# Counting SyncE's row fetches on one semaphore per batch, and giving SyncE 16 batches to fetch in place of 12

## The chip, the cores and the metric

The kernel runs on one core of a Trainium2 chip. A core has a matrix engine (TensorE, PE in the profile; its weight loads are PEld), a vector engine (VectorE, DVE), an activation engine (ScalarE, ACT), GpSimd (POOL) and SyncE (SP), which computes nothing and issues transfers. Each engine works through a list of instructions in the order in which they were written, and engines wait for one another through semaphores. ScalarE, SyncE and GpSimd can issue DMA transfers; the transfers of all three run on the core's 16 DMA engines. The metric is the device time of one execution in microseconds (us); lower is better.

## The reference

A layer of a graph network: 12,500 nodes with 160 features each, 400,000 edges, sorted by destination. The part that matters here is the gather of a mapped node row for each edge, the product with weights that each edge computes for itself, and the sum by destination.

```python
h = jnp.maximum(_layernorm(x, axis=-1), 0.0)
y0 = x0 @ W_l1_0 * a * inv0                       # y: one row of 160 floats per node
y1 = jnp.einsum('nuc,uv->nvc', x1, W_l1_1) * a[:, :, None] * inv1
w = silu(edge_length_embedded @ fc_W1 / 4) @ fc_W2 / 8    # weights of each edge
ys0 = y0[edge_src]                                # the gather
ys1 = y1[edge_src]
mid_a = w_a * ys0 * e0
mid_b = (w_b * ys0)[:, :, None] * e1[:, None, :]
...
z0 = jnp.zeros((n, MID)).at[edge_dst].add(mid0) * inv_nb
out = x + concat(C_S * s0 + C_X * (z0 @ W_l2_0) * a / sqrt(MID), ...)   # s0: the node's own path
```

## The kernel before, in words

A first stage maps all nodes and writes the rows to `y_d` in HBM. Then the main loop goes over the edges in 782 batches (`NB`) of 4 tiles (`GT`) of 128 edges, so a batch needs 512 rows of `y_d`, 640 bytes each. The loop takes almost all of the time. For each batch PE computes the edges' weights (L689), DVE builds the selection of destinations (L704, L706) and the products of weights and rows (L573, L577), and PE sums the products by destination (L720).

The order of every engine's instructions is the order in which the program text issues them (`manual_schedule`); nothing is moved afterwards. So a batch's steps stand on each engine in the order of the loop body, and an engine that waits holds up all that stands behind it.

The rows of a batch come in one of four ways:

- GpSimd fetches them with four indirect gathers, one for each tile (L615), into a ring of 6 buffers (`yg`). This is the way of most batches.
- 18 batches (`XB`), one in every 43 (`PER`), get raw features early and are mapped again on PE (`x_center`, `x_turn`, `x_map`), in the 18 slots of the buffer `xr`. A slot is free for other use once its x batch is done.
- SyncE fetches all 512 rows of a batch one by one: each row is one small DMA from `y_d` into the slot (`row_fetch_by_sp`, L638), whose address SyncE reads from SBUF into registers, 32 at a time (`row_places`, L626, one TENSOR_LOAD). The table `jobs` says which batches. A job starts in batch `s`, spreads its 16 chunks of 32 rows over the next `RB` = 58 batches, and its rows are used 7 batches after that; the next job starts `RB` after the one before. 12 jobs.
- ScalarE does the same in units of 8 rows, one unit at the end of a batch's steps (`row_fetch_by_act`); its jobs stand `AB` = 66 apart. 10 jobs.

SyncE also issues the loads of edge features `xe` (L407, two every 8 batches), of edge attributes and indices `raw`, `src_q`, `dst_q` (L415 to L419) and one store `drel_d` (L433) every 24 batches, and of the nodes' own features `xs` for the nodes' own path (L766, three in every 43 batches). These stand in the same list as the row fetches. DVE reads `xs` at L773 (`skip_center`), five batches behind the load's place in the program at the closest.

Semaphores: the framework counts a DMA of SyncE or ScalarE in one of eight *lanes* (DMAHW0 to DMAHW7), taken in turn; a DMA waits until the one before it in its lane has landed. ScalarE's rows are excepted already: they count on a semaphore of their own for each batch (`came`, `no_tile_sem_insts`, `add_to_no_dep_group`), and DVE waits for that semaphore's full count (`all_rows`) ahead of the batch's first product. SyncE's rows use the lanes.

Of the kernel before, what the change touches and what calls it, by code (L numbers as in the profile page):

```python
# [12 lines left out]
U8 = mybir.dt.uint8  # L13
# [9 lines left out]
D = M0 + 3 * M1  # L23
# [20 lines left out]
LATE = 8  # L44
XB = 18
SK = 9
RB = 58
RS = 30
AB = 66
AS = 102  # L50
RN = 32
AN = 16
RU = 8
# [7 lines left out]
def kernel(  # L61
# [19 lines left out]
    nc = tc.nc  # L81
# [10 lines left out]
    for q, w in enumerate(wts_of):  # L92
        gstart.append(len(glist))
        n = min(BLK, T - q * BLK)
# [9 lines left out]
    y_b = y_d.rearrange("n c -> (n c)").bitcast(U8)  # L104
# [51 lines left out]
    NX = P * GT // RN  # L156
    jobs = [(s, RB, True) for s in range(RS, NB - 1 - RB - 7, RB)]
    jobs += [(s, AB, False) for s in range(AS, NB - 1 - AB - 7, AB)]
    jobs = [(s, s + m + 7, m, by_sp) for s, m, by_sp in sorted(jobs)]
# [420 lines left out]
    with (  # L580
# [10 lines left out]
        hids, rows, wts, sels, z_ps, zT, o_sb, prs, sums_ps, summed = ({} for _ in range(10))  # L591
        xss, hss, sTs, sps, ohs, ohTs, vals, xTs = ({} for _ in range(8))
        halves, came, places_of = {}, {}, {}
# [30 lines left out]
        def row_places(j, n, m, engine):  # L624
            q, o = divmod(n, P // RP * GT)
            _, places = nc.values_load_multi_w_load_instructions(  # L626
                ri[RP * j + q:RP * j + q + 1, o:o + m], engines=[engine], min_val=0, max_val=(N - 1) * D * 4,
                skip_runtime_bounds_check_because="places of nodes, as the indices of the other fetches")
            return places

        def row_fetch(j, n, eng, places):
            b = jobs[j][1]
            if n == 0:
                rows[b] = xr[:, slot_of[j], :, :]
            fetches = []
            for m, v in enumerate(places):
                e, k = divmod(n + m, GT)
                fetches.append(eng.dma_start(rows[b].bitcast(U8)[e:e + 1, k, :], y_b[ds(v, D * 4)].unsqueeze(0)))  # L638
            return fetches

        def row_fetch_by_sp(j, n):
            row_fetch(j, RN * n, nc.sync, row_places(j, RN * n, RN, mybir.EngineType.SP))

        def row_fetch_by_act(j, n):
            o = RU * n % AN
            if n == 0:
                came[jobs[j][1]] = tc.alloc_semaphore(f"rows_{j}"), f"rows_{j}"
            sem, group = came[jobs[j][1]]
            for fetch in row_fetch(j, RU * n, nc.scalar, places_of[j][o:o + RU]):
                fetch.then_inc(sem, 16)  # L650
                tc.no_tile_sem_insts.add(fetch.ins.name)
                tc.add_to_no_dep_group(group, fetch.ins)

        def act_places(j, n):
            if RU * n % AN == 0:
                places_of[j] = row_places(j, RU * n, AN, mybir.EngineType.Activation)

        def all_rows(b):
            if b in came:
                sem, group = came[b]  # L660
                tc.declare_fence(nc.vector.wait_ge(sem, 16 * P * GT).ins, group=group)
# [289 lines left out]
        for b in range(NB):  # L951
            g = group_of[b]
            k = b - first_of[g]
# [9 lines left out]
            u, v = divmod(b, PER)  # L963
# [3 lines left out]
            if units and units[0][0] <= b:  # L967
                act_places(*units[0][1:])
# [27 lines left out]
            if units and units[0][0] <= b:  # L996
                row_fetch_by_act(*units.pop(0)[1:])
# [12 lines left out]
    with (  # L1010
# [4 lines left out]
        n = nc.values_load(far_i[0:1, 0:1], min_val=0, max_val=1)  # L1015
        with tc.For_i(0, n, 1) as _:
# [77 lines left out]
            with tc.For_i(0, NT, 1) as i:  # L1094
# [4 lines left out]
                for c in range(3):  # L1099
                    o = 256 + 64 * c  # L1100
# [62 lines left out]
```

## Time and profile before

| | |
|---|---|
| median of 3 runs | 4903.42 us |
| lowest, highest | 4900.01, 4938.69 us |
| the profiled execution | 4914.76 us |
| its span in the profile | 4912.9 us |
| busy: PE, DVE, POOL, ACT | 3930.2, 2747.3, 2878.2, 609.6 us |
| rows fetched by SyncE, by ScalarE | 6144, 5120 |
| gathers by GpSimd (L615) | 2965 |

The profile names work by engine and by line of the kernel before. A row of the view of waits gives who waited for whom, the total in us, how often, and the longest. A row of the timeline gives the start in us, the length in us, the engine (SPq and ACTq are the parts of SyncE and ScalarE that issue transfers), the line, the operation and how many instructions of it were merged.

### The profile page before, as it was taken

The numbers are of one execution on the slowest core, as the hardware profiler recorded it, in microseconds if no ns is written. First come the engines' busy times: TensorE is split into PE (matmuls) and PEld (weight loads), VectorE is DVE, ScalarE is ACT, GpSimd is POOL, SyncE is SP. The second block draws the span as 40 slices with busy tenths as digits, with TensorE's granted clock in tenths as the row PEclk, the third lists the DMA queues.
The fourth block names the chain that finished last, engine by engine and source line by source line (L and its number), as shares of the span: only waits on it lengthen the run. The fifth ranks groups of instructions, "written<-read, shape, count | busy, mean of one in ns | idle before, by whom it ended". The sixth has DMA issues, their size and how long they took to land. (4 is left out here: it accounts for less than half of the span.)

```text
span 4912.9 us, 76368 instructions
## 1 busy us (share of the span) xinstructions
PE 3930.2 (80%) x17274; PEld 2517.5 (51%) x17274; DVE 2747.3 (56%) x6901; ACT 609.6 (12%) x1863; POOL 2878.2 (59%) x3045
## 2 busy tenths in 40 slices
PE   7778887767778686887777787888887888888888
PEld 7444544444445454554454555555554555555555
DVE  5455555544555454555455565566565666666666
ACT  5011011101101010111011111111111111111110
POOL 6666665646656565555556556566556555565654
PEclk8889898878989898988899898899898888999889
DMA  7222222222222222222222222222222222222223
GB/s 194 67 69 64 70 66 64 60 55 65 65 57 65 58 66 59 64 61 61 56 64 65 63 57 66 61 67 64 64 60 64 61 65 61 65 63 62 65 61 109
DMA packets 272510, 330.52 MB, mean 67 GB/s; under 512 B 84288, under 2 KB 223456, under 8 KB 272048
## 3 DMA queue, kind: packets, MB, share of 16 engines
q0 software_dynamic: 145776, 248.99, 20.5%
q1 hardware_dynamic: 115408, 73.03, 5.3%
q10 hardware_dynamic: 10864, 3.57, 0.4%
q8 instruction: 140, 2.29, 0.2%
q14 instruction: 322, 2.64, 0.2%
HBM read 307.72 MB, written 17.61 MB: 66 GB/s over the span
## 5 line engine op out<-in xcount | busy, mean ns | idle before, releaser
L615 POOL DMA_INDIRECT yg<-y_d,src_q x2965 | 2808.5, 947 | 1962.4 <-issue 702.5
L720 PE MATMUL pz<-pr,sel 128*128 128x320 f32 x6250 | 2122.9, 486 | 51.4 <-issue 23.2
L720 PEld LDWEIGHTS pz<-pr,sel 128*128 128x128 f32 x6250 | 1244.4, 210 | 726.2 <-issue 384.3
L689 PE MATMUL pw<-w,hT 64*128 64x192 f32 x6250 | 825.4, 387 | 331.4 <-DVE pr L577 168.3
L689 PEld LDWEIGHTS pw<-w,hT 64*128 64x128 f32 x6250 | 567.4, 210 | 632.0 <-issue 512.1
L726 DVE STREAM_TRANSPOSE za<-pz 128x160 f32<-128x160 f32 x598 | 206.2, 345 | 1050.5 <-PE pz L720 443.5
L577 DVE TENSOR_TENSOR pr<-pw,yg 128x384 f32<-128x384 f32 x1484 | 749.4, 546 | 0.0
L706 DVE TENSOR_TENSOR sel<-own,pw 128x512 f32<-128x512 f32 x782 | 536.8, 686 | 28.3 <-DVE own L704 1.4
L573 DVE TENSOR_TENSOR pr<-pw,yg 128x512 f32<-128x512 f32 x742 | 506.2, 682 | 9.3 <-DMA yg<-y_d,src_q 9.3
L704 DVE TENSOR_TENSOR own<-iota,pw 128x128 f32<-128x128 f32 x782 | 204.8, 262 | 511.2 <-issue 265.3
L668 PE MATMUL px<-xe,w 32*128 32x512 f32 x782 | 442.1, 648 | 40.5 <-issue 15.9
L568 ACT ACTIVATE pw<-ev 128x20 f32<-128x20 f32 x782 | 149.2, 191 | 2472.6 <-DMA xr<-y_d 526.1
L673 ACT ACTIVATE hT<-px 128x512 f32<-128x512 f32 x391 | 233.2, 597 | 972.4 <-remote 220.5
L733 PEld LDWEIGHTS px<-wo,za 128*128 128x128 f32 x1500 | 227.4, 203 | 153.2 <-issue 77.6
L733 PE MATMUL px<-wo,za 128*128 128x160 f32 x1500 | 261.5, 325 | 53.0 <-issue 11.9
L668 PEld LDWEIGHTS px<-xe,w 32*128 32x128 f32 x782 | 115.6, 185 | 220.0 <-issue 180.4
L745 PE MATMUL px<-os,place 128*128 128x160 f32 x600 | 127.7, 340 | 116.6 <-ACT os L735 94.6
L727 DVE STREAM_TRANSPOSE za<-pz 32x160 f32<-32x160 f32 x598 | 202.0, 338 | 21.6 <-DVE za L726 1.2
L780 PE MATMUL px<-ident,sh 128*128 128x128 f32 x98 | 31.7, 341 | 219.7 <-DVE sh L773 180.3
L745 PEld LDWEIGHTS px<-os,place 128*128 128x128 f32 x600 | 100.0, 209 | 163.2 <-ACT os L735 114.5
L773 DVE TENSOR_SCALAR sh<-xs,mv 128x160 f32<-128x160 f32 x98 | 26.5, 309 | 251.9 <-DMA xs<-in_x 251.9
L780 PEld LDWEIGHTS px<-ident,sh 128*128 128x128 f32 x98 | 15.9, 163 | 241.0 <-issue 176.4
(129 smaller groups left out, 1623.7 us busy)
## 6 DMA issues: line engine op xcount, KB each, us to landing
xr<-y_d SPq DMA_DIRECT2D x6144, 0.6 KB
xr<-y_d ACTq DMA_DIRECT2D x5120, 0.6 KB
yg<-y_d,src_q POOLq DMA_INDIRECT x2965
xe<-in_e SPq DMA_DIRECT2D x196, 128.0 KB
xs<-in_x SPq DMA_DIRECT2D x48, 160.0 KB
acc<-in_x SPq DMA_DIRECT2D x11, 640.0 KB
y_d<-ys SPq DMA_DIRECT2D x11, 640.0 KB
out<-acc SPq DMA_DIRECT2D x11, 640.0 KB
```

Source lines behind the costliest of these rows:

```text
L573: nc.vector.tensor_mul(pr[:, :n, :].rearrange("p t (x u) -> p t x u", x=2)[:, :, :, 0:M0], wt[:, :n, 0:NW].rearrange("p t (x u) -> p t x u ...
L577: nc.vector.tensor_mul(pr[:, :n, D * x + M0:D * (x + 1)].rearrange("p t (c u) -> p t c u", c=3), wt[:, :n, 96 * x + M0:96 * (x + 1)].unsqu ...
L615: fetch = nc.gpsimd.indirect_dma_start(out=yg[:, slot(t), :], out_offset=None, in_=y_d, in_offset=bass.IndirectOffsetOnAxis(ap=ev4[t // BL ...
L668: nc.tensor.matmul(ph, w1[r, :], xe[r, :], start=True, stop=True)
L673: nc.scalar.activation(hT, ph, AF.Silu, scale=1.0 / math.sqrt(FC_IN))
L689: nc.tensor.matmul(pw[:, k, 0:NW], hT[r, o:o + P], w2[r, :], start=True, stop=True)
L704: nc.vector.tensor_tensor(own[:, :n, :], iota[:, 0:WN].unsqueeze(1).to_broadcast([P, n, WN]), wt[:, :n, NW + 4:NW + 5].to_broadcast([P, n, ...
L706: nc.vector.tensor_tensor(sel, own[:, :n, :].unsqueeze(2).to_broadcast([P, n, 4, WN]), wt[:, :n, NW:NW + 4].unsqueeze(3).to_broadcast([P, ...
L720: mm = nc.tensor.matmul(pz[:, 0:PC], sel[:, slot(t), :, :], pr[:, slot(t), :], start=o == 0, stop=last)
L726: nc.vector.transpose(zT[g][:, :, at_w], pz[:, D:PC].rearrange("p (k u) -> p k u", k=ZK))
L733: nc.tensor.matmul(po[:m, :], za[:, k, :m], wo[:, k, :], start=k == 0, stop=k == ZK - 1)
L745: nc.tensor.matmul(ps[:, h, :], place[:m, h, :], os[:m, :], start=True, stop=True)
```

## The change

SyncE's row fetches leave the lanes: like ScalarE's they count on the batch's own semaphore, and the code for that moves from `row_fetch_by_act` into `row_fetch`, which both use. DVE now waits for that semaphore in all 26 batches that are fetched row by row, not in 10. A table of numbers changes with it: SyncE's jobs start in batch 26, not 30, and stand 44 apart, not 58, so that there are 16 and not 12; ScalarE's ten start in batch 108, not 102, and stand 65 apart, not 66. Lines behind L650 stand three lower.

```diff
-RB = 58
-RS = 30
-AB = 66
-AS = 102
+RB = 44
+RS = 26
+AB = 65
+AS = 108
...
             if n == 0:
                 rows[b] = xr[:, slot_of[j], :, :]
-            fetches = []
+                came[b] = tc.alloc_semaphore(f"rows_{j}"), f"rows_{j}"
+            sem, group = came[b]
             for m, v in enumerate(places):
                 e, k = divmod(n + m, GT)
-                fetches.append(eng.dma_start(rows[b].bitcast(U8)[e:e + 1, k, :], y_b[ds(v, D * 4)].unsqueeze(0)))
-            return fetches
-
-        def row_fetch_by_act(j, n):
-            o = RU * n % AN
-            if n == 0:
-                came[jobs[j][1]] = tc.alloc_semaphore(f"rows_{j}"), f"rows_{j}"
-            sem, group = came[jobs[j][1]]
-            for fetch in row_fetch(j, RU * n, nc.scalar, places_of[j][o:o + RU]):
+                fetch = eng.dma_start(rows[b].bitcast(U8)[e:e + 1, k, :], y_b[ds(v, D * 4)].unsqueeze(0))
                 fetch.then_inc(sem, 16)
                 tc.no_tile_sem_insts.add(fetch.ins.name)
                 tc.add_to_no_dep_group(group, fetch.ins)

+        def row_fetch_by_act(j, n):
+            o = RU * n % AN
+            row_fetch(j, RU * n, nc.scalar, places_of[j][o:o + RU])
```

The list of SyncE from the `xs` load of program batch 119 to the next, in batch 128. Each row is an instruction, with its line, what it writes and reads, and how many alike follow. Before:

```order
L766 DMA xs<-in_x 128x2x160
L407 DMA xe<-in_e 128x1x256 x2
L626 TENSOR_LOAD ri
L638 DMA xr<-y_d 1x640 x32
L433 DMA drel_d<-drel 128x96
L626 TENSOR_LOAD ri
L638 DMA xr<-y_d 1x640 x32
L766 DMA xs<-in_x 128x2x160
```

The same stretch of SyncE's list in the changed kernel:

```order
L763 DMA xs<-in_x 128x2x160
L626 TENSOR_LOAD ri
L639 DMA xr<-y_d 1x640 x32
L407 DMA xe<-in_e 128x1x256 x2
L626 TENSOR_LOAD ri
L639 DMA xr<-y_d 1x640 x32
L433 DMA drel_d<-drel 128x96
L626 TENSOR_LOAD ri
L639 DMA xr<-y_d 1x640 x32
L626 TENSOR_LOAD ri
L639 DMA xr<-y_d 1x640 x32
L763 DMA xs<-in_x 128x2x160
```

Between the same two loads stood two chunks of 32 rows, and now stand four; over 43 batches it is 384 rows before and 480 to 512 now.

The waits in SyncE's list around one `xs` load, before (what a row waits for stands in brackets; DMAHW0 to DMAHW7 are the lanes):

```order
L638 DMA xr<-y_d 1x640 [waits DMAHW6_49]
L638 DMA xr<-y_d 1x640 [waits DMAHW7_49]
L766 DMA xs<-in_x 128x2x160 [waits DMAHW0_49]
L407 DMA xe<-in_e 128x1x256 [waits DMAHW1_49,PE_49]
L407 DMA xe<-in_e 128x1x256 [waits DMAHW2_49]
L626 TENSOR_LOAD ri
L638 DMA xr<-y_d 1x640 [waits DMAHW3_49]
```

And around one such load in the changed kernel, where rows without a bracket wait for nothing:

```order
L626 TENSOR_LOAD ri
L639 DMA xr<-y_d 1x640 x32
L407 DMA xe<-in_e 128x1x256 [waits DMAHW2_49,PE_49]
L407 DMA xe<-in_e 128x1x256 [waits DMAHW3_49]
L626 TENSOR_LOAD ri
L639 DMA xr<-y_d 1x640 x32
L763 DMA xs<-in_x 128x2x160 [waits DMAHW6_49,DMAHW4_49,DVE_49]
```

The row fetches lost their waits; the loads between them kept theirs, on lanes that hold loads alone.

DVE's list at the first batch that SyncE fetched, before:

```order
L704 TENSOR_TENSOR own<-iota,pw 128x128 [waits Activation_49]
L706 TENSOR_TENSOR sel<-own,pw 128x512 [waits DVE_49]
L573 TENSOR_TENSOR pr<-pw,xr 128x8x64 [waits DMAHW4_49,DMAHW5_49,DMAHW3_49,DMAHW6_49,DMAHW2_49,DMAHW7_49,DMAHW1_49,DMAHW0_49]
L577 TENSOR_TENSOR pr<-pw,xr 128x4x96 x2
```

And in the changed kernel:

```order
L701 TENSOR_TENSOR own<-iota,pw 128x128 [waits rows_0,Activation_49]
L703 TENSOR_TENSOR sel<-own,pw 128x512 [waits DVE_49]
L573 TENSOR_TENSOR pr<-pw,xr 128x8x64 [waits DVE_sequencer_49]
L577 TENSOR_TENSOR pr<-pw,xr 128x4x96 x2
```

The wait for the rows moved two instructions ahead, from the product to the comparison that opens the batch's work.

More of the change, by code (lines that the diff above doesn't have):

```diff
@@ L634, in row_fetch @@
                 rows[b] = xr[:, slot_of[j], :, :]
-            fetches = []
+                came[b] = tc.alloc_semaphore(f"rows_{j}"), f"rows_{j}"
+            sem, group = came[b]
             for m, v in enumerate(places):
                 e, k = divmod(n + m, GT)
-                fetches.append(eng.dma_start(rows[b].bitcast(U8)[e:e + 1, k, :], y_b[ds(v, D * 4)].unsqueeze(0)))
-            return fetches
-        def row_fetch_by_sp(j, n):
-            row_fetch(j, RN * n, nc.sync, row_places(j, RN * n, RN, mybir.EngineType.SP))
-        def row_fetch_by_act(j, n):
-            o = RU * n % AN
-            if n == 0:
-                came[jobs[j][1]] = tc.alloc_semaphore(f"rows_{j}"), f"rows_{j}"
-            sem, group = came[jobs[j][1]]
-            for fetch in row_fetch(j, RU * n, nc.scalar, places_of[j][o:o + RU]):
+                fetch = eng.dma_start(rows[b].bitcast(U8)[e:e + 1, k, :], y_b[ds(v, D * 4)].unsqueeze(0))
                 fetch.then_inc(sem, 16)
@@ L652, in row_fetch_by_act, with row_fetch_by_sp @@
                 tc.add_to_no_dep_group(group, fetch.ins)
+        def row_fetch_by_sp(j, n):
+            row_fetch(j, RN * n, nc.sync, row_places(j, RN * n, RN, mybir.EngineType.SP))
         def act_places(j, n):
```

## The prediction

> **What bounds the kernel now.** I read the page first, then the view of waits, then SyncE's own waits, then SyncE's timeline over one turn of 43 batches. The page names no engine that is busy throughout:
>
> ```profile
> PE 3930.2 (80%) x17274; PEld 2517.5 (51%) x17274; DVE 2747.3 (56%) x6901; ACT 609.6 (12%) x1863; POOL 2878.2 (59%) x3045
> xr<-y_d SPq DMA_DIRECT2D x6144, 0.6 KB
> xr<-y_d ACTq DMA_DIRECT2D x5120, 0.6 KB
> ```
>
> Issuing does not count as busy, so SyncE has no share there at all. The view of waits shows it at second hand, and the view of SyncE's waits (650 to 4500 us) from its own side:
>
> ```profile
> DVE sh L773 <- DMA xs<-in_x: 251.9, 18, 29.8
> PE px L780 <- DVE sh L773: 180.3, 15, 28.1
> ...
> SPq L638 <- DMA xr<-y_d: 64.8, 133, 1.4
> SPq L626 <- DVE own L704: 2.1, 1, 2.1
> ```
>
> DVE waited 251.9 us for the nodes' own features, PE behind it. But SyncE, which loads them, waited hardly at all: 64.8 us for lanes in 3850, the next row of that view is 2.1. An engine that never waits and whose loads come late is one with too long a list. Its timeline over one turn, from one `xs` load to the same one 43 batches on, says so (the eight groups of rows, the two loads at the ends):
>
> ```profile
> 2149.49 0.01 SPq L766 DMA_DIRECT2D xs<-in_x  x1
> 2151.43 23.00 SPq L638 DMA_DIRECT2D xr<-y_d  x32
> ...
> 2178.26 21.45 SPq L638 DMA_DIRECT2D xr<-y_d  x32
> ...
> 2202.59 15.07 SPq L638 DMA_DIRECT2D xr<-y_d  x32
> ...
> 2223.30 37.93 SPq L638 DMA_DIRECT2D xr<-y_d  x64
> ...
> 2265.96 47.71 SPq L638 DMA_DIRECT2D xr<-y_d  x64
> ...
> 2317.51 23.38 SPq L638 DMA_DIRECT2D xr<-y_d  x32
> ...
> 2343.66 43.71 SPq L638 DMA_DIRECT2D xr<-y_d  x64
> ...
> 2392.55 40.82 SPq L638 DMA_DIRECT2D xr<-y_d  x64
> ...
> 2434.69 0.48 SPq L766 DMA_DIRECT2D xs<-in_x  x1
> ...
> L626 SPq TENSOR_LOAD <-ri x192: 14/2118/2501, 255.2 to 4566.3; - x192
> ```
>
> The turn is 2434.69 - 2149.49 = 285.2 us. It holds 384 rows in 253.07 us. Twelve reads of places at 2.118 us (the median in the last row) are 25.4; four of them lie inside the groups of 64, so rows alone cost (253.07 - 8.5) / 384 = **0.637 us**, and 285.2 - 244.6 - 25.4 = 15.2 us is other loads. The list has no gap: here SyncE sets the pace, and DVE's waits for `xs` are how the rest is held to it. The mean turn, over 13 of them:
>
> ```profile
> 811.41 0.42 SPq L766 DMA_DIRECT2D xs<-in_x  x1
> ...
> 4257.08 0.69 SPq L766 DMA_DIRECT2D xs<-in_x  x1
> ```
>
> (4257.08 - 811.41) / 13 = **265.1 us**.
>
> **What a row's price depends on.** The same SyncE, with its lanes, in the longest wait of DVE, once GpSimd has fallen silent (its last gather starts at 1074.01):
>
> ```profile
> 1094.82 0.52 DVE L773 TENSOR_SCALAR sh<-xs,mv 128x160 f32<-128x160 f32 x2 [29.77 <-DMA xs<-in_x]
> ...
> 1074.01 0.95 POOL L615 DMA_INDIRECT yg<-y_d,src_q  x1 [0.30 <-issue]
> ...
> 1081.54 10.67 SPq L638 DMA_DIRECT2D xr<-y_d  x32
> ```
>
> 32 rows in 10.67 us are **0.333 us** a row. In a run of eight gathers back to back, first and last below, it is 7 rows in 8.55 us, 1.22 each. ScalarE, whose rows use no lane, takes 8.62 us for 8 at the same moment; its other groups around it are quoted with it:
>
> ```profile
> 2126.11 0.94 POOL L615 DMA_INDIRECT yg<-y_d,src_q  x1 [1.44 <-PE px L668]
> ...
> 2134.87 0.95 POOL L615 DMA_INDIRECT yg<-y_d,src_q  x1 [0.30 <-issue]
> ...
> 2128.30 8.55 SPq L638 DMA_DIRECT2D xr<-y_d  x7
> ...
> 2115.17 2.73 ACTq L638 DMA_DIRECT2D xr<-y_d  x8
> ...
> 2121.05 2.40 ACTq L638 DMA_DIRECT2D xr<-y_d  x8
> ...
> 2126.06 2.68 ACTq L638 DMA_DIRECT2D xr<-y_d  x8
> ...
> 2128.95 8.62 ACTq L638 DMA_DIRECT2D xr<-y_d  x8
> ...
> 2139.16 2.64 ACTq L638 DMA_DIRECT2D xr<-y_d  x8
> ...
> 2142.39 7.70 ACTq L638 DMA_DIRECT2D xr<-y_d  x8
> ```
>
> So the price follows GpSimd's gathers, not the lanes. One more row speaks for that: after a pause in which all earlier rows had landed, the first 8 rows still took 4.82 us (0.60 each) beside gathers, though eight lanes were free but for the store just issued:
>
> ```profile
> 365.44 0.42 SPq L766 DMA_DIRECT2D xs<-in_x  x1
> 372.73 0.38 SPq L433 DMA_DIRECT2D drel_d<-drel  x1
> 375.35 4.82 SPq L638 DMA_DIRECT2D xr<-y_d  x8
> ```
>
> **The change, part by part.**
>
> *Four more batches on SyncE.* A turn of 43 batches holds 43 x 512 / 58 = 379.6 rows before and 43 x 512 / 44 = 500.4 after: 120.8 more, and 3.8 more reads of places (8.0 us). SyncE has no idle time to put them in, so the turn grows. GpSimd's gathers in a turn stay as many, so the added time is time in which GpSimd has run dry, and the added rows go at the price beside a silent GpSimd: 120.8 x 0.333 + 8.0 = **48.3 us** a turn. The other bound takes the mean of the turn, 253.07 / 384 = 0.659 with its reads: 80 us. I take the first, because the waits that will grow are of the kind at 1094.82, whose second part went at that price. SyncE's jobs cover batches 26 to 730, 704 / 43 = 16.4 turns; I take 15, since SyncE begins ahead and must first use that up. 15 x 48.3 = +724 us (at 80: +1200).
>
> *No lanes for SyncE's rows.* Each row loses a wait. What they cost in the whole run is a row of SyncE's waits:
>
> ```profile
> SPq L638 <- DMA xr<-y_d: 81.3, 167, 1.4
> ```
>
> SyncE is the bound, so all of it counts: -81 us; the lower end of the gain is zero, since a landed row may have been named where something else held SyncE. The upper end is the first rival.
>
> *Sixteen gathers fewer on GpSimd* (4 batches of 4, 0.95 + 0.30 us each by the rows above): 20 us of an engine that is not waited for; nothing. If GpSimd were the bound, they would be worth those 20 us.
>
> *The wait on DVE in 16 batches*, two instructions ahead of where it was. `own` and `sel` stand behind it now, under 1 us by the busy rows of L704 and L706, and only where rows are late. Rows are issued 7 batches before use, more than the 5 batches after which a late `xs` load stops DVE; so `xs` is the wait that ends last, and this costs nothing. Without that cover it is 16 us.
>
> *ScalarE's ten jobs, 65 apart:* still 10 x 64 units of 8; each batch has at most one. Nothing, either way.
>
> Sum: 4914.8 + 724 - 81 = 5558 us for the profiled execution, which stands 11 us over the median of 4903.4. On that scale **5550 us**. With the high price 6030, and with fewer turns at the silent price of the 13 that I could count (13 x 48.3 - 81) 5450; a little below that if SyncE works off more ahead. Own range of this case: 5350 to 6000.
>
> **The rivals.**
>
> *The lanes were the limit.* If a row waited for the row eight before it in the runs of gathers, that wait goes and every row costs 0.333 us. A turn then takes SyncE 500.4 x 0.333 + 15.6 x 2.118 + 15.2 = 215 us, less than 265.1; DVE's 251.9 us of waits go, and the time is 4903 - 252 = 4650, or 4780 with half of them gone. It decides from a row price of (265.1 - 48.2) / 500.4 = 0.433 us on down; under 0.427 it is faster by over 1%. For it: ScalarE, without lanes, mostly shows 8 rows in 2.4 to 2.7 us. Against it: 0.333 with lanes, 8.62 without. The Trainium skill ("DMA: Bandwidth & Descriptors", section "Latency and other measured facts") speaks for it: an HBM access takes 0.2 us on average and 2 us at high load, and is the larger part of a small DMA's fixed 2 us. By that rule a row's landing beside gathers would take some 4 us (an estimate from that page), eight in flight would give 0.5 us a row, and most of the sum above would turn round. The group at 375.35 speaks against it: its rows were that dear with nothing in flight. Chance 0.24.
>
> *ScalarE's price.* The six groups of ScalarE above are 48 rows in 26.77 us, 0.558 each. If being without lanes makes the difference to 0.637, SyncE saves 379.6 x 0.079 = 30 us of the 48 in a turn: 4915 + 15 x 18.3 = 5190. ScalarE pauses between groups, which SyncE does not, and that explains the difference as well. Chance 0.12.
>
> *Break-even.* The price falls to about 0.433, and the added rows eat what the cheaper ones save: 4850 to 4950. Chance 0.08.
>
> **How the numbers follow.** Price unchanged 0.56, ScalarE's price 0.12: slower 0.68. Break-even 0.08: within 1%, about what a measurement of this kernel can tell from no change. Lanes 0.24: faster. The range runs from 4780, which leaves out somewhat over half of the last case, to 6000, which leaves out the high price alone.
>
> **What would show it.** Right: L770 (`sh`, L773 before) waits for `xs` 900 us or more in all, in nearly every one of its 45 places; SyncE's timeline is still without gaps; 32 rows still take over 20 us beside gathers; PE's busy share falls towards 70%. Wrong: groups of 32 rows in 10 to 13 us beside gathers, gaps in SyncE's list, no wait at `sh`. Then the lanes held SyncE, in a way that the view of waits does not charge to them.

## The result, and the profile after

On the chip of the kernel before, the changed kernel took 5593.26 us, the median of 4 runs (5584.20 to 5618.48); the kernel before took 4911.00 there (also the median of 4, 4900.01 to 4938.69). The ratio is **1.1407**, with a 95% interval from 1.1363 to 1.1450: slower by 14%. The forecast was 5550 us, in a range from 4780 to 6000. The profiled execution after took 5584.20 us, its span is 5582.4; that of before was 4912.9, so the two spans differ by 669.5.

The page after, its line of busy times:

```profile
PE 3953.0 (71%) x17274; PEld 2523.5 (45%) x17274; DVE 2749.2 (49%) x6902; ACT 607.8 (11%) x1863; POOL 2869.6 (51%) x3029
```

And the view of waits (us in all, times, longest):

```profile
DVE sh L770 <- DMA xs<-in_x: 817.7, 29, 52.1
PE px L777 <- DVE sh L770: 705.1, 31, 48.6
...
DVE neg L196 <- DMA dst_q<-in_dst: 185.8, 10, 28.4
PE px L665 <- DMA xe<-in_e: 74.9, 7, 19.7
DVE own L701 <- DMA xr<-y_d: 10.6, 2, 9.0
```

PE, DVE and POOL are busy for as long as before, within 23 us; what grew is waiting. The waits for `xs` rose from 251.9 to 817.7 us, and two loads that did not stand among the larger waits before, `dst_q` and `xe`, now hold DVE and PE as well. All three loads are on SyncE's list. The rows themselves (`xr`), for which the change put a fence on DVE, are waited for 10.6 us.

SyncE's own waits, the largest two between 650 and 5100 us, show that it is never held:

```profile
SPq L407 <- PE pz L717: 2.4, 4, 0.7
SPq L407 <- DMA xe<-in_e: 2.0, 4, 1.0
```

And its timeline over one turn of 43 batches, rows and `xs` loads alone, from one `xs` to the third after it, is without gaps again:

```profile
2202.09 0.41 SPq L763 DMA_DIRECT2D xs<-in_x  x1
2204.73 32.28 SPq L639 DMA_DIRECT2D xr<-y_d  x64
2240.88 15.18 SPq L639 DMA_DIRECT2D xr<-y_d  x32
2256.15 0.42 SPq L763 DMA_DIRECT2D xs<-in_x  x1
2258.82 45.27 SPq L639 DMA_DIRECT2D xr<-y_d  x64
2307.90 18.12 SPq L639 DMA_DIRECT2D xr<-y_d  x32
2328.90 18.46 SPq L639 DMA_DIRECT2D xr<-y_d  x32
2353.53 58.67 SPq L639 DMA_DIRECT2D xr<-y_d  x96
2415.34 35.83 SPq L639 DMA_DIRECT2D xr<-y_d  x96
2451.23 0.41 SPq L763 DMA_DIRECT2D xs<-in_x  x1
2455.47 31.05 SPq L639 DMA_DIRECT2D xr<-y_d  x64
2489.10 19.69 SPq L639 DMA_DIRECT2D xr<-y_d  x32
2509.13 0.41 SPq L763 DMA_DIRECT2D xs<-in_x  x1
```

This turn takes 2509.13 - 2202.09 = 307.0 us and holds 512 rows; the short stretches between the lines are reads of places and other loads. Groups of 32 rows take 15 to 20 us here, where three of four took over 21 in the turn shown of before: GpSimd is silent for more of the turn, and rows that fall there are cheap. The same two `xs` loads that gave the mean turn before (thirteen turns apart) give it after:

```profile
881.71 0.42 SPq L763 DMA_DIRECT2D xs<-in_x  x1
...
4912.34 0.42 SPq L763 DMA_DIRECT2D xs<-in_x  x1
```

(4912.34 - 881.71) / 13 = 310.0 us, against 265.1 before: 44.9 us more a turn. With the reads at 2.118 us and 15.2 us of other loads taken off, a row cost (265.1 - 15.2 - 25.1) / 379.6 = 0.592 us before and (310.0 - 15.2 - 33.1) / 500.4 = 0.523 after.

### The profile page after: what moved, and what is told of

Same layout as the page of the kernel before. It is cut to its first block, busy times and chain, and to the rows that moved or that the text cites. A ratio compares the mean times of both kernels' runs of the same rounds, so it can differ in the third digit from the quotient of the medians.

```text
span 5582.4 us, 80448 instructions
## 1 busy us (share of the span) xinstructions
PE 3953.0 (71%) x17274; PEld 2523.5 (45%) x17274; DVE 2749.2 (49%) x6902; ACT 607.8 (11%) x1863; POOL 2869.6 (51%) x3029
## 3 DMA queue, kind: packets, MB, share of 16 engines
q0 software_dynamic: 145008, 247.67, 17.9%
## 4 chain that ended last, share of the span: by engine, by line
SPq 19%; PE 17%; issue 13%; DVE 3%; another core or an unknown queue 2%; ACTq 1%; DMA 1%; POOL 0%; ACT 0%; DVEq 0%; POOLq 0%
SPq L639 16%; PE pz L717 9%; PE pw L686 3%; SPq L626 3%; PE px L665 2%; PE px L730 1%; DVE pr L577 1%; ACTq L639 1%; PE px L742 1%; SPq L407 1%; POOL yg L615 0%; DMA xs<-in_x 0%; DVE pr L573 0%; DVE za L723 0%
## 5 line engine op out<-in xcount | busy, mean ns | idle before, releaser
L665 PE MATMUL px<-xe,w 32*128 32x512 f32 x782 | 449.6, 657 | 112.3 <-DMA xe<-in_e 74.9
L568 ACT ACTIVATE pw<-ev 128x20 f32<-128x20 f32 x782 | 149.3, 191 | 2619.5 <-PE pz L717 607.7
L770 DVE TENSOR_SCALAR sh<-xs,mv 128x160 f32<-128x160 f32 x98 | 25.6, 301 | 817.9 <-DMA xs<-in_x 817.7
L730 PE MATMUL px<-wo,za 128*128 128x160 f32 x1500 | 260.7, 324 | 21.1 <-issue 12.9
```

The lines of the kernel that those rows point to most:

```text
L665: nc.tensor.matmul(ph, w1[r, :], xe[r, :], start=True, stop=True)
L730: nc.tensor.matmul(po[:m, :], za[:, k, :m], wo[:, k, :], start=k == 0, stop=k == ZK - 1)
```

## The experiments

They ran on three further chips, and a ratio is always to the kernel before on the same chip. It took 4996.49 us on the second, 4914.03 on the third and 3840.57 on the fourth. That last number is itself a finding; the last section comes back to it. Ranges in us in the expectations of the four runs on the second chip are on the first chip's scale, so there the ratios count.

**The theories.** A, the one on record: SyncE's list is full, a row's price is set by GpSimd's gathers, and the new table alone makes the loss. B: the lanes held SyncE. C: something else in the change (the ScalarE table, the place of a load in the list) matters.

### The parts of the change alone (second chip)

`nolane58` takes the new semaphores with the old table, so in the changed kernel:

```
-RB = 44   RS = 26   AB = 65   AS = 108
+RB = 58   RS = 30   AB = 66   AS = 102
```

> The semaphores of the change alone: SyncE's rows leave the lanes, the 12 jobs stay 58 apart. Theory A (SyncE's list is full and GpSimd's gathers set the price of a row): the lane waits of 81 us at most come back, 4830 to 4911 us; DVE's waits for xs fall from 252 to 170 us or more; a group of 32 rows still takes over 20 us beside gathers. Theory B (the lanes set the price): 4650 us, no waits for xs. Theory C (the new semaphores themselves cost, by DVE's wait ahead of the batch or by SyncE's counting): over 5000 us.

Measured: 4974.59 us, ratio 0.9945 (0.9913 to 0.9977). The ratio is where theory A had it. Without lanes SyncE's rows no longer wait, but the waits for `xs` are as long as before:

```profile
DVE sh L770 <- DMA xs<-in_x: 269.3, 16, 28.5
```

So at 58 apart the semaphores alone gain 0.55%, 27 us on the first chip's scale, and on this chip the lanes were not the limit.

`lane44` is the other half, the old lanes with the new table, so in the kernel before:

```
-RB = 58   RS = 30   AB = 66   AS = 102
+RB = 44   RS = 26   AB = 65   AS = 108
```

> The table of the change alone: 16 jobs of SyncE 44 apart, ScalarE's 65 apart, rows still in lanes. Theory A: 5593 us plus up to 110 us for lane waits (81 us x 8192/6144), 5590 to 5700. Theory C: under 5200, since the added rows were not what cost. If lanes cost more the denser the rows stand: over 5750.

Measured: 5687.88 us, ratio 1.1362 (1.1292 to 1.1431), with these waits:

```profile
DVE sh L773 <- DMA xs<-in_x: 849.4, 30, 57.6
```

The table alone makes the whole loss that can be measured, at the lower edge of theory A's range. Its interval holds the 1.1407 of the changed kernel, so at 44 apart the lanes cannot be priced between chips.

`act65` has only ScalarE's new table in the kernel before (`AB = 65`, `AS = 108`).

> ScalarE's part of the table alone in the kernel before: its ten jobs start in batch 108 and stand 65 apart. Theory A: no difference, 4860 to 4960 us. If ScalarE's places had a part in the loss: over 4960.

Measured: 5005.76 us, ratio 1.0026 (0.9996 to 1.0056). No difference that can be measured; that part of C falls.

### Fewer gathers (second and third chip)

`half_gathers` leaves out the gathers of every second batch in the changed kernel; those batches read one fixed tile of zeros:

```
+            if b % 2 and b >= AHEAD:
+                rows[b] = still
+                return
```

> The changed kernel with every second batch of GpSimd's gathers left out (their products read a tile of zeros; the ring of gather buffers has 5, for room). Theory A: SyncE's list is unchanged, but a row costs near 0.333 us in most of the time, the list of a turn takes 215 to 250 us, and the time falls to 4600 to 4900 us; the waits for xs shrink to under 300 us. If a row's price is SyncE's own whatever GpSimd does: over 5400 us, with the waits for xs as they are.

Measured: 4076.89 us, ratio 0.8148 (0.8098 to 0.8197), much faster than either theory had it. The granted clock was 0.933 against 0.837, and the zeros could have been the reason, so `half_gathers2`, on the third chip, fills that tile once with a batch of real rows (both have 5 gather buffers in place of 6):

```
+        for k in range(GT):
+            t = AHEAD * GT + k
+            nc.gpsimd.indirect_dma_start(out=still[:, k, :], ...)
```

> The changed kernel with every second batch's gathers left out, as in half_gathers, but those batches now read one batch of real rows that was gathered once, not zeros (its output is not the reference's). It asks whether half_gathers was fast because SyncE's rows became cheap, or because zeros let the chip grant TensorE a higher clock. Theory A (rows get cheap where gathers come in short runs): the clock falls back from 0.933 towards 0.88, groups of 32 rows on SyncE still take 10 to 14 us, DVE's waits for xs stay under 300 us, and the time is 4200 to 4500 us. Rival B (the zeros and the clock made the gain): groups of 32 rows go back to 15 to 23 us, the waits for xs to over 600 us, and the time to 4900 us or more.

Measured: 4063.81 us, ratio 0.8260 (0.8238 to 0.8282), at the same clock. The zeros did nothing, and I was wrong to suspect them. SyncE's timeline of `half_gathers2`, with the row of the cores and its wait for `xs`:

```profile
core 0: 4065.1 us, clock 0.933
```

```profile
2088.17 0.42 SPq L768 DMA_DIRECT2D xs<-in_x  x1
2090.89 24.14 SPq L644 DMA_DIRECT2D xr<-y_d  x64
...
2174.56 11.57 SPq L644 DMA_DIRECT2D xr<-y_d  x32
```

```profile
DVE sh L775 <- DMA xs<-in_x: 442.5, 29, 33.3
```

32 rows take 11.57 us and 64 take 24.14: (24.14 - 2.118) / 64 = 0.344 a row. It is so everywhere: in thirteen turns no chunk of 32 takes more than 12.6 us. Taking gathers away makes rows cheap, with SyncE's list as long as in the changed kernel. What I missed was the size: I had waits for `xs` under 300 us, and they are 442.5, because everything else got faster too, and SyncE, at its 512 rows a turn, is again what the rest waits for.

### The order of the list, or its length (third chip)

`xs_by_act` has ScalarE issue the loads of `xs`:

```
-            node_dma(t, m, lambda rows, k, p: nc.sync.dma_start(xs[:p, k, :], ...))
+            node_dma(t, m, lambda rows, k, p: nc.scalar.dma_start(xs[:p, k, :], ...))
```

> The changed kernel with one line altered: ScalarE issues the loads of xs, SyncE everything else as before. Theory A (SyncE's whole list is too long, and xs is merely where that shows first): the time stays at 5300 to 5650 us, the waits for xs fall under 150 us, and about as much comes up as waits of the DVE fence on the rows, of PE for xe and of DVE for dst_q, which are still on SyncE's list. Rival B (only the place of xs behind groups of rows in the list hurts, and the rows themselves have time): the time falls under 5000 us, since the rows are fetched 7 batches ahead of use, and no other wait takes over.

Measured: 5573.32 us, ratio 1.1349 (1.1307 to 1.1391). The waits for `xs` are gone from the top of the view, and others have their place:

```profile
DVE neg L196 <- DMA dst_q<-in_dst: 480.0, 20, 35.8
...
DVE own L701 <- DMA xr<-y_d: 394.9, 16, 43.4
...
PE px L665 <- DMA xe<-in_e: 196.7, 17, 19.0
```

Together 1071.6 us, as in the changed kernel: 817.7 + 185.8 + 74.9 = 1078.4. It is the length of the list that costs; which load is named is only which stands where the lag shows first. The rows are late too: DVE waits 394.9 us for them at the fence once the wait for `xs` is gone. As the total stays, this isn't a price of the fence; what the fence costs by standing two instructions ahead was not measured.

### A shorter list (third chip)

`rb72` gives SyncE 10 batches instead of 16 in the changed kernel (`RB = 72`, `RS = 30`, `AB = 66`, `AS = 102`).

> The changed kernel with SyncE's batches 72 apart (10 of them) in place of 44 (16), ScalarE's ten 66 apart. A turn of 43 batches then holds 306 rows on SyncE in place of 380 at 58 apart, so at 0.61 us a row, 10 reads of places at 2.1 and 15 us of other loads it takes SyncE 223 us, less than the 251 us that a turn takes without waits for xs. Theory A (SyncE's list sets the pace): the waits for xs fall from the 269 us of nolane58 to under 100, and the time to 4700 to 4850 us on a chip where the kernel before takes 4910, a ratio of 0.955 to 0.985. Rival B (GpSimd's gathers set the pace, and rows on SyncE are a relief for them): 8 more gathers than before at 1.25 us make it 10 us slower than nolane58, a ratio of 0.995 to 1.005.

Measured: 4753.18 us, ratio **0.9657** (0.9627 to 0.9686): faster than the kernel before, as theory A had it. SyncE now waits for work, and the wait for `xs` has left the view's first 60 rows. SyncE's waits between 650 and 4500 us:

```profile
SPq L433 <- DVE za L723: 91.2, 7, 19.4
SPq L433 <- DVE drel L261: 83.5, 6, 20.9
```

The view of all waits has a large row that no spacing removes:

```profile
ACT pw L568 <- issue: 574.2, 205, 9.0
```

ScalarE waits 574.2 us for nothing that the profile shows, in 205 places. In the changed kernel on the first chip this row is as large, 559.7 us in 200 places.

### Number of gathers, or their bytes (third chip)

`thin` keeps every gather and its 128 places, with 64 bytes a place in place of 640; DVE reads three columns of each row:

```
+            c = D if b < AHEAD else 16
-                    out=yg[:, slot(t), :], out_offset=None, in_=y_d,
+                    out=yg[:, slot(t), 0:c], out_offset=None,
+                    in_=y_d if c == D else y_d.rearrange("n (a c) -> (n a) c", c=16),
```

> The changed kernel with gathers of the same number and the same 128 places each, but 64 bytes a place in place of 640; DVE's products read columns 0 to 2 of each row in place of all 160 (its output is not the reference's). It asks what of the gathers makes SyncE's rows dear. Theory A1 (their number: GpSimd's and the rings' work for 128 places each): groups of 32 rows beside gathers still take 15 to 23 us, the waits for xs stay over 600 us, the time 5300 to 5650 us. Theory A2 (their bytes: 82 KB each through DMA engines and HBM): groups of 32 rows fall to 10 to 13 us everywhere, the waits for xs under 200 us, the time under 4700 us.

Measured: 5644.30 us, ratio 1.1481 (1.1445 to 1.1517). Its queue of gathers (packets, MB, share) moved 32.02 MB in 98208 packets, where that of the changed kernel moved 247.67 in 145008:

```profile
q0 software_dynamic: 98208, 32.02, 5.6%
```

Its timeline and its wait for `xs` are those of the changed kernel:

```profile
2029.64 62.79 SPq L641 DMA_DIRECT2D xr<-y_d  x96
...
2206.46 15.45 SPq L641 DMA_DIRECT2D xr<-y_d  x32
```

```profile
DVE sh L772 <- DMA xs<-in_x: 832.2, 30, 53.9
```

This is theory A1. An eighth of the bytes, in two thirds of the packets, makes no row cheaper. What makes a row dear goes with the gathers themselves, not with the bytes that they carry.

### The lanes at 44, and two more spacings (fourth chip)

`after2` is the changed kernel again.

> The changed kernel once more, side by side with the kernel before and with lane44b, so that the lanes can be priced at 44 apart on one chip. Both theories: a ratio to the kernel before of 1.135 to 1.145.

`lane44b` is `lane44` again.

> The kernel before, with its lanes, and the changed table alone (44, 26, 65, 108). Theory A (lanes cost only the waits that the profile charges to them, 65 to 100 us before, of which 27 came back in nolane58): 0 to 40 us longer than after2. Rival (lanes hold SyncE in a way that the waits do not show, and more so with more rows): more than 100 us longer than after2.

`rb50` has 14 batches on SyncE (`RB = 50`, `RS = 26`, `AB = 66`, `AS = 102`).

> The changed kernel with SyncE's batches 50 apart (14 of them), ScalarE's 66 apart: a turn of 43 batches holds 440 rows of SyncE, 60.7 more than at 58 apart, and 1.9 more reads of places. Theory A (SyncE is full from 58 on, each further row adds the silent price): 60.7 x 0.333 + 4 = 24.2 us a turn, x 15 turns = +363 us, less the 27 of the lanes: a ratio of 1.055 to 1.08. Rival (a threshold lies between 58 and 44, where a lag that has been harmless runs out): a ratio under 1.03 or over 1.10.

`rb88` has 8 (`RB = 88`, `RS = 30`, `AB = 66`, `AS = 102`).

> The changed kernel with SyncE's batches 88 apart (8 of them), ScalarE's 66 apart. Theory A (at 72 apart SyncE has slack already, its list sets nothing any more): two more batches by gathers, 8 gathers of 1.25 us, give at most 10 us: the same as rb72 to 15 us longer, a ratio of 0.963 to 0.971. Rival (fewer rows on SyncE go on paying): another 30 us or more off, a ratio under 0.960.

Theory A missed in all four, because on this chip the kernel before takes 3840.57 us and the price of a row is another. In `lane44b` and `rb50` the number fell on the rival's side; in `rb88` both missed:

| kernel | us | ratio to before, 95% |
|---|---|---|
| `after2` | 3937.99 | 1.0257 (1.0240 to 1.0274) |
| `lane44b` | 4100.57 | 1.0674 (1.0657 to 1.0692) |
| `rb50` | 3829.82 | 0.9973 (0.9963 to 0.9982) |
| `rb88` | 3862.19 | 1.0058 (1.0041 to 1.0075) |

The timeline of `after2`, of GpSimd and then of SyncE at the same moment, and the first and last `xs` of the same thirteen turns:

```profile
2027.88 0.95 POOL L615 DMA_INDIRECT yg<-y_d,src_q  x1 [0.30 <-PE pz L717]
...
2050.72 0.95 POOL L615 DMA_INDIRECT yg<-y_d,src_q  x1 [0.30 <-issue]
```

```profile
2027.52 23.30 SPq L639 DMA_DIRECT2D xr<-y_d  x64
```

```profile
643.90 0.42 SPq L763 DMA_DIRECT2D xs<-in_x  x1
...
3427.41 0.42 SPq L763 DMA_DIRECT2D xs<-in_x  x1
```

```profile
DVE pr L573 <- DMA yg<-y_d,src_q: 356.1, 180, 5.3
...
DVE sh L770 <- DMA xs<-in_x: 225.5, 22, 26.0
```

Beside 19 gathers back to back (first and last above), 64 rows and a read take 23.30 us, (23.30 - 2.118) / 64 = 0.331 a row: the price that the first chip showed when GpSimd was silent. The list still sets the pace at 44 apart, though by little: DVE now waits for gathers as well (356.1 us, 9.5 on the first chip). 500.4 rows at 0.331, 15.6 reads at 2.118 and 15.2 us make 213.9 us a turn; measured are (3427.41 - 643.90) / 13 = 214.1.

Here the lanes count. `lane44b` is 4100.57 - 3937.99 = 162.6 us longer than `after2`, and SyncE waits for lanes (here between 650 and 3600 us; 121.9 in the whole run) and DVE for `xs`:

```profile
SPq L638 <- DMA xr<-y_d: 113.7, 277, 1.4
```

```profile
DVE sh L773 <- DMA xs<-in_x: 392.8, 25, 34.5
```

At 50 apart a turn takes less, by the same two `xs` loads of `rb50`:

```profile
631.37 0.41 SPq L763 DMA_DIRECT2D xs<-in_x  x1
...
3281.27 0.42 SPq L763 DMA_DIRECT2D xs<-in_x  x1
```

(3281.27 - 631.37) / 13 = 203.8 us, in which 440.3 rows, 13.8 reads and 15.2 us fill 190. Then the gathers set the pace: in the thirteen turns of `rb50`, and of `rb88`, they follow one another with no pause over 0.6 us, and the largest DMA wait is DVE's for them, first in `rb50`, then in `rb88`.

```profile
DVE pr L573 <- DMA yg<-y_d,src_q: 537.6, 307, 6.0
```

```profile
DVE pr L573 <- DMA yg<-y_d,src_q: 624.4, 354, 5.4
```

`rb88` has 24 gathers more than `rb50`; at 1.25 us that is 30 us, and 3862.19 - 3829.82 = 32.4 were measured. So on this chip fetching more batches by rows does pay, down to about 50 apart. Against the kernel before, `rb50` gains 0.3%, and part of that may be its missing lanes: 58 apart without lanes was not run here.

## Why the prediction held, point by point

**SyncE's list is full and sets the pace.** Shown. With six batches fewer on it the waits for `xs` vanish (`rb72`), and with `xs` off it the same 1070 us come up elsewhere (`xs_by_act`).

**Added rows go at the price beside a silent GpSimd, 48.3 us a turn.** The step held closely. The turn grew by 44.9 us with the lanes' gain in it. That gain, if it is what `nolane58` shows, is 27 us in 16.4 turns, 1.6 a turn, so rows and reads added 46.5. Less the 8.0 for the reads, an added row cost 38.5 / 120.8 = 0.319 us, where 0.333 was taken, while the mean row cost 0.523. The two traces also show where the added rows went. This is a count over the thirteen turns, by the time from one row's start to the next (steps over 1.9 us, with a read or a load between, left out); a row is beside gathers while gathers stand less than 0.6 us apart:

| a turn of | rows beside gathers | us each | rows in GpSimd's silence | us each | time with gathers, us |
|---|---|---|---|---|---|
| before | 231.5 | 0.703 | 130.4 | 0.355 | 192.3 |
| after | 246.9 | 0.677 | 234.6 | 0.339 | 193.7 |

Of some 120 added rows 104 fell into the silence, and the time with gathers stayed. The added work ran while the engine that makes a row dear had run dry.

**Fifteen turns.** (669.5 + 27) / 46.5 = 15.0, and 669.5 / 44.9 = 14.9 without the lanes' part. The number held, its reason did not. A head start of SyncE would show as early turns without a loss, but the first load of the thirteen turns is already 881.71 - 811.41 = 70.3 us late, and behind the last one only 669.5 - 655.3 = 14.2 us are added.

**The lanes, -81 us.** This term was mis-sized. `nolane58` gives -27 us (-11 to -43 by its interval), a third of it. That is at 58 apart; at 44 it was not measured on a chip with dear rows. The likely reading, not shown by itself, is that SyncE would have been held anyway in most of the 81.3 us that the view charges to lanes. The text had zero as the lower end for this reason, and then took the upper.

**16 gathers fewer, the fence on DVE, ScalarE 65 apart: nothing.** Held: the rows were waited for 10.6 us in all at the fence, and `act65` shows no difference. On the fourth chip, where GpSimd sets the pace, gathers are worth their 1.25 us each.

The sum was 643 us over before (724 - 81); the spans differ by 669.5, the medians by 682. Two errors ran against each other: 28 us too many for the rows, 54 too many for the lanes. That the sum comes so close is in part luck.

**What would show it.** No gaps in SyncE's list and PE at 71%: as written. "L770 waits for `xs` 900 us or more, in nearly every one of its 45 places" was not: 817.7 in 29 places, and 260.7 more at `dst_q` and `xe`. The prediction took the list's lag to show at one load, and it shows at whichever load is next. "32 rows still take over 20 us beside gathers" held for the rows that are beside gathers (32 x 0.677 = 21.7). But with GpSimd silent for more of the turn, only 62 of 204 chunks of 32 in the thirteen turns take over 20 us, where before it was 68 of 154.

**The rival that the lanes were the limit.** It fell on the chip that was predicted, and on the second by `nolane58`: its rows wait for no landing and still cost 0.710 us beside gathers and 0.356 in the silence, counted as in the table above, much as the 0.703 and 0.355 of the kernel before. The Trainium skill ("DMA: Bandwidth & Descriptors", "Latency and other measured facts") spoke for the rival, with an access to HBM that goes from 0.2 us on the mean to 2 at high load. No run here timed such an access; but as `nolane58` doesn't wait for landings, their length is not what makes its rows dear. On the fourth chip, where rows cost 0.331 without lanes, the lanes do hold SyncE. Eight rows in flight at that price cover 2.6 us, and a landing that takes longer stops the list; at 0.6 a row they cover 4.8. This mechanism is worked out from the prices; no run timed a single landing. Even there the change as a whole is slower, by 2.6%: the new list takes 214 us a turn, much as the rival had it (215), but the rest of the kernel then needs only about 204, the turn of `rb50`. The rival had kept the rest at the pace of a chip on which the rest was slow too.

**The rivals of ScalarE's price and of break-even.** Both had rows get cheaper for want of lanes. By `nolane58` they don't. The mean row did fall, to 0.523 us, but by the silence into which the added rows fell.

**What stays open.** From `half_gathers2` I had formed a further theory: on the third chip its gathers run in pairs, while before and after most runs hold four, six or eight, and rows turn dear from about the third gather of a run on (in the kernel before 0.43 and 0.52 us a row beside the first two, 0.88 and 1.08 beside the next two). The fourth chip contradicts it as a sufficient cause: `after2` has a run of 966 gathers, from 97 to 1309 us, with no pause over 1.5 us, and its rows beside gathers cost 0.331 on the mean. So on three of four chips gathers made rows dear, and on one they did not. Why is not settled; each chip was measured at one time only, so a property of the chip and a state that it was in can't be told apart. Spacings of 50 and 88 were not tried on a chip with dear rows, nor 72 on the fourth.

## What to carry to other kernels

An engine that issues and never waits, while others wait for its loads, is the bound, though no busy share shows it; price a longer list for it by what an added item costs once everyone else has stopped, not by the mean item. Wait time charged to a resource does not tell what removing it brings: of 81.3 us charged to lanes 27 came back where rows were dear, and where they were cheap 162.6 came back for 121.9. A table that balances two engines fits the chip on which it was tuned: the changed kernel, 44 apart, lost 14% on one chip and 2.6% on another, so check a balance on more than one.

## What the runs showed of the hardware that was not expected

**The same program on another chip took 22% less.** (4914.03 - 3840.57) / 4914.03 = 0.218. It isn't the work of DVE or POOL: in the changed kernel DVE was busy 2749.2 us on the first chip and 2750.7 on the fourth, POOL 2869.6 and 2871.9. What differs in the traces is the time between instructions. On the first chip the trace has steps of about 0.7 and 1.4 us between SyncE's instructions in the stretches of gathers, and ScalarE's at the same moments. They strike register moves, which start no transfer, as much as DMA issues: of SyncE's 4771 moves for rows between 650 and 3600 us 487 took over 0.5 us, the longest 1.48, and of its 4771 DMA issues 509. Among 6914 moves on the fourth chip the longest took 0.04. So it is not only the issuing of DMAs that is late. The Trainium skill ("Runtime: NRT & Kernel Launch", "Instruction fetch mechanics") says that a sequencer fetches its instructions by a DMA queue of its own, in blocks of 256, and that this is mostly hidden. A late block would then make one pause in 256 instructions. In this trace, from the fourth gather of a run on, 778 of 1333 instructions of SyncE's row fetches were followed by the next only after more than 0.5 us; a late block alone does not explain that, and no run here tells what does.

**The loss reaches further than SyncE's list.** `rb72` has slack on SyncE and still takes 4753.18 us, where `rb88` on the fourth chip takes 3862.19 with more gathers. ScalarE's waits at L568 for nothing that the profile shows are 559.7 us in the changed kernel on the first chip and 125.1 on the fourth; that the same steps make them is likely, but not shown.

**The granted clock goes with PE's busy share, not with the data or the chip.** Eight of the profiled executions over all chips, in order of span:

| kernel | span us | PE busy | clock |
|---|---|---|---|
| `rb50` | 3818.8 | 93% | 0.974 |
| `after2` | 3935.0 | 91% | 0.955 |
| `half_gathers2` | 4065.1 | 88% | 0.933 |
| `half_gathers` (zeros) | 4072.3 | 88% | 0.933 |
| `rb72` | 4750.6 | 82% | 0.900 |
| before | 4912.9 | 80% | 0.883 |
| after | 5582.4 | 71% | 0.837 |
| `lane44` | 5686.3 | 70% | 0.832 |

Zeros and real rows have the same clock, and so have kernels of like busy share on different chips (`lane44b` on the fourth: 87%, 0.938). PE's own work took longer where the clock was lower: it was busy 3953.0 us in the changed kernel on the first chip (0.837) and 3578.0 on the fourth (0.955), for the same 17274 instructions. That fits waits of PE being paid a second time at a lower clock; no run set the one without the other.
